# RWKV6 stage of a one-core hybrid layer: mixing on ACT and POOL, r times k on VectorE, other places for parts of PE's work and for the sends, the first fills from SBUF, weights from ACT's queue

## The chip, the core and the metric

The kernel runs on one core of a Trainium2 chip. Its engines are TensorE (PE, with its weight loads, PEld), VectorE (DVE), ScalarE (ACT), GpSimd (POOL) and SyncE (SP), which here only issues transfers. Each engine works through its own instructions in order; semaphores tie them together. The metric is the device time of one execution in microseconds, and lower is better.

## What is computed

The input x has 4 sequences of 1024 tokens with 256 channels, all in fp32. Four sublayers follow one another, each as `x = x + f(layernorm(x))`: a retention attention, a mixture of experts (MoE: 8 experts, the best two of a softmax router, SiLU-gated), an RWKV6 attention, and the same MoE with the same weights again. The change is in the RWKV6 sublayer and in its handover to the second MoE. Cut to what matters, RWKV6 is:

```
sx  = shift(x) - x                               # shift: the token before
m   = tanh((x + sx * maa_x) @ tm_w1)             # 5 parts of 32 columns
xf  = x + sx * (maa[f] + m[f] @ tm_w2[f])        # f = 0..4: w, k, v, r, g
r, k, v, g = x3 @ Wr, x1 @ Wk, x2 @ Wv, silu(x4 @ Wg)
w   = exp(-exp(decay + tanh(x0 @ td_w1) @ td_w2))
# for each of 16 heads (16 x 16 state), token by token:
y_t = r_t . (state + u * k_t v_t)
state = w_t * state + k_t v_t
out = (groupnorm(y) * ln_w + ln_b) * g @ Wo
```

The term `r . (u * k v)` does not need the state. The kernel computes it apart, as `bonus = v * sum(u * r * k)`.

## The kernel before

**Stages.** Retention comes first (0 to about 350 us of the profiled execution). The first MoE follows as two halves of 2048 tokens, 39 slots of 128 rows each. RWKV6's block 0 is prepared during the second half (`prepare`, lists `first`). RWKV6 then runs until about 1358 us. The second MoE ends the program.

**RWKV6.** The 4096 tokens are 8 blocks of 512 (`NBLK`, block j; two blocks make one sequence). In a block, 8 slots n = 0..7 of two runs h = 0, 1 cover the 256 x 16 state rows. This text counts slots over the whole stage too: slot 8j + n. For each run:

- `fill` (L926 to 937) brings the values of v, spread over partitions, from a DRAM copy (`v_all`, written by `store`, L915) into a tile `w_vb` (3 buffers), by SP's queue. It is issued two runs ahead.
- `run` (L951) is the core: on DVE a product k*v (L957, 128x1024) and two scans (L959, 128x512 each) that carry the state along 512 tokens; on POOL the product with r (L967). The tiles `w_s` have 6 buffers. Parts given as `between` go on DVE between the two scans.
- `sums` (L980) adds the state rows on PE into `w_yp`, one slot later.

`factors` (L908) makes the tile `w_wk` of one half g of the channels on ACT: `exp(-ew)` and a copy of k. Slots 0 to 3 use g = 0, slots 4 to 7 use g = 1 in the scans.

**The next block, in between.** While block j runs, block j+1 is prepared piece by piece: `normed`, `turn` (transposes; sx on POOL), `mix` (tanh), `both` (products `w_dp` on PE, L842, then `mixed`, L845 to 856, which makes each `w_xf`), `decay`, `decay2` and `projected` (L880). Block j-1 is finished at the same time: `centre`, `spread`, `root`, `spread_out`, `gated`, `out_part`, `added`. The lists `given`, `amid`, `late` and `uses` (L1074 to 1112) are written out by hand and say in which slot each part is emitted: `uses` between the scans of the slot's first run, `amid` after that run, `late` at the slot's end, and `given[n, h]` after the other run of slot n.

**The second MoE's router and rows.** For each finished block, `block` takes statistics, `logits` (L491) transposes the normed rows and multiplies with the router into `m_lp`, and `biased` (L504) adds the bias on DVE. `route` runs one of 8 pieces of small DVE operations that sort the rows to experts. `send` (L634) makes one tile of rows on ACT and scatters it to DRAM by two indirect DMAs of POOL. The main loop (L1367 to 1391) puts these into slots, and loads the expert weights `w1a` and `w2a` (4 and 2 MB, `load`, L1251) by SP's queue in the slots 58 to 63, after the pool `pi`, which held the tiles of RWKV6's preparation, has been released.

**Order.** PE and ACT, and in these stages DVE and POOL too, run in the order in which the program emits their instructions. Only SP's order, which holds nothing but transfers, is laid by a planner.

## Time and profile before

| | us |
|---|---|
| runs: median of 3 (lowest, highest) | 1650.17 (1642.9, 1650.6) |
| the profiled execution: its own time | 1690.56 |
| its span, from the first to the last instruction | 1688.7 |
| RWKV6: first to last running product and scan | 698.1 to 1358.1 |
| second MoE: first matmul on fetched rows | 1368.5 |

The profile shows one execution, and it took 2.4% longer than the median of the runs. Sums over its rows are therefore sums against 1690.56. A row of a group gives the line, the engine, the operation, the tiles, the shapes and the count, then the busy time and the mean of one in ns, then the idle time just before and what ended it. A row of the waits names who waited for whom, the total, the number of times and the longest. A row of the windows gives the busy time of each engine in a stretch of the span.

### The profile page before, as it was taken

The numbers are of one execution on the slowest core, as the hardware profiler recorded it, in microseconds if no ns is written. First come the engines' busy times: TensorE is split into PE (matmuls) and PEld (weight loads), VectorE is DVE, ScalarE is ACT, GpSimd is POOL, SyncE is SP. The second block draws the span as 40 slices with busy tenths as digits, with TensorE's granted clock in tenths as the row PEclk, the third lists the DMA queues.
The fourth block names the chain that finished last, engine by engine and source line by source line (L and its number), as shares of the span: only waits on it lengthen the run. The fifth ranks groups of instructions, "written<-read, shape, count | busy, mean of one in ns | idle before, by whom it ended". The sixth has DMA issues, their size and how long they took to land. (4 is left out here: it accounts for less than half of the span.)

```text
span 1688.7 us, 21332 instructions
## 1 busy us (share of the span) xinstructions
PE 1418.5 (84%) x6800; PEld 747.9 (44%) x6800; DVE 1002.8 (59%) x1874; ACT 608.8 (36%) x1451; POOL 925.2 (55%) x879
## 2 busy tenths in 40 slices
PE   6999998858989999888898889878876467989993
PEld 4666665635555555322333333323322134555662
DVE  6666556414323532597978897889976824423534
ACT  2343334323343333424343434432425133433331
POOL 4233323632455344698969696966797732464331
PEclk9999988879999999979878787877877758999997
DMA  8921111132333421666545343533445910333625
GB/s 305 334 67 51 55 47 54 62 113 74 98 118 124 145 65 56 152 161 152 148 112 137 98 128 98 137 88 93 119 119 144 270 58 32 101 123 123 207 92 174
DMA packets 111882, 204.11 MB, mean 121 GB/s; under 512 B 12224, under 2 KB 73632, under 8 KB 111776
## 3 DMA queue, kind: packets, MB, share of 16 engines
q1 hardware_dynamic: 93920, 161.07, 33.5%
q0 software_dynamic: 17856, 41.70, 7.9%
q8 instruction: 58, 0.95, 0.2%
q14 instruction: 48, 0.39, 0.1%
HBM read 142.27 MB, written 60.45 MB: 120 GB/s over the span
## 5 line engine op out<-in xcount | busy, mean ns | idle before, releaser
L967 POOL TENSOR_TENSOR w_s<-w_s,w_rT 128x1024 f32<-128x1024 f32 x128 | 304.2, 2394 | 92.3 <-DVE w_s L959 88.6
L708 POOL DMA_INDIRECT y_all<-m_y,m_to x156 | 151.0, 968 | 328.5 <-ACT m_xt L663 191.4
L668 PE MATMUL m_hp<-w1a,m_xt 128*128 x624 | 311.4, 623 | 11.7 <-ACT m_xt L663 10.3
L674 DVE TENSOR_TENSOR m_a<-m_hp,m_sg 128x256 f32<-128x256 f32 x156 | 66.2, 424 | 352.7 <-ACT m_sg L672 320.9
L702 PE MATMUL m_op<-w2a,m_aT 128*128 x624 | 165.2, 388 | 13.7 <-ACT m_y L707 11.2
L957 DVE TENSOR_TENSOR w_vb<-w_vb,w_wk 128x1024 f32<-128x1024 f32 x128 | 153.9, 1202 | 37.2 <-DMA w_vb<-v_all 20.9
L959 DVE TENSOR_TENSOR_SCAN w_s<-w_wk,w_carry,w_vb 128x512 f32<-128x512 f32 x128 | 160.2, 1275 | 7.8
L959 DVE TENSOR_TENSOR_SCAN w_s<-w_wk,w_vb 128x512 f32<-128x512 f32 x128 | 152.0, 1215 | 7.4
L668 PEld LDWEIGHTS m_hp<-w1a,m_xt 128*128 128x128 f32 x624 | 112.1, 200 | 94.6 <-issue 82.8
L640 POOL DMA_INDIRECT xg_all<-m_row,m_at x128 | 124.7, 974 | 51.9 <-issue 30.0
L672 ACT ACTIVATE m_sg<-m_hp 128x256 f32<-128x256 f32 x156 | 59.9, 384 | 174.2 <-PE m_hp L668 143.9
L707 ACT ACTIVATE m_y<-m_op,m_share 128x256 f32<-128x256 f32 x156 | 73.8, 473 | 133.4 <-PE m_op L702 85.4
L702 PEld LDWEIGHTS m_op<-w2a,m_aT 128*128 128x128 f32 x624 | 108.0, 193 | 28.7 <-ACT m_y L707 17.4
L297 POOL TENSOR_TENSOR a_t<-a_t,a_t 128x512 f32<-128x512 f32 x32 | 41.1, 1285 | 124.8 <-DVE a_t L296 114.7
L990 PE MATMUL w_yp<-w_s,core_c 128*32 128x512 f32 x512 | 91.0, 711 | 10.9 <-POOL w_s L967 10.7
L842 PE MATMUL w_dp<-w_m,tm_w2a 32*128 32x512 f32 x128 | 75.5, 837 | 17.3 <-DVE w_cen L1044 7.4
L856 POOL TENSOR_TENSOR w_xf<-w_xf,w_xT 128x512 f32<-128x512 f32 x80 | 86.1, 1091 | 4.2 <-DVE w_xf L852 0.4
L695 PEld LDWEIGHTS m_atp<-cst,m_a 128*128 128x128 f32 x312 | 44.1, 144 | 92.8 <-issue 74.0
L327 DVE TENSOR_TENSOR a_pt<-a_sp,ret_c 128x2048 f32<-128x2048 f32 x32 | 73.1, 2286 | 17.8 <-PE a_sp L324 17.7
L663 ACT COPY m_xt<-m_xtp 128x256 f32<-128x256 f32 x156 | 57.0, 366 | 48.5 <-PE m_xtp L659 45.9
L659 PE MATMUL m_xtp<-cst,m_xg 128*128 128x128 f32 x312 | 63.0, 286 | 13.5 <-DMA m_xg<-xg_all 13.0
L697 DVE COPY m_aT<-m_atp 128x256 f32<-128x256 f32 x156 | 64.9, 416 | 5.2 <-PE m_xtp L659 2.9
(226 smaller groups left out, 2480.1 us busy)
## 6 DMA issues: line engine op xcount, KB each, us to landing
w_vb<-v_all SPq DMA_DIRECT2D x128, 512.0 KB
m_xg<-xg_all SPq DMA_DIRECT2D x36, 520.0 KB
tab<-in_rope SPq DMA_DIRECT2D x32, 512.0 KB
m_back<-y_all SPq DMA_DIRECT2D x48, 256.0 KB
xg_all<-zero SPq DMA_DIRECT2D x18, 520.0 KB
w1a<-in_w SPq DMA_DIRECT2D x16, 512.0 KB
v_all<-w_vT SPq DMA_DIRECT2D x64, 128.0 KB
res<-in_x SPq DMA_DIRECT2D x8, 512.0 KB
```

What stands on the lines that cost most here:

```text
L327: nc.vector.tensor_mul(pts[i].rearrange("p j n t -> p (j n) t"), sp.rearrange("p j n t -> p (j n) t"), causal.unsqueeze(1).to_broadcast([P ...
L640: nc.gpsimd.indirect_dma_start(out=xg_views[self.half][2 * i + n][:, :], out_offset=bass.IndirectOffsetOnAxis(ap=self.at[n][:, i : i + 1], ...
L668: mm(hp, lhsT=self.xt[j][:, c, :], rhs=w1a[:, bass.ds(self.ev[j], 1), c, :].rearrange("p o n -> p (o n)"), start=(c == 0), stop=(c == KC - 1))
L702: mm(op, lhsT=self.aT[j][:, c, :], rhs=w2a[:, bass.ds(self.ev[j], 1), c, :].rearrange("p o n -> p (o n)"), start=(c == 0), stop=(c == KC - 1))
L707: nc.scalar.activation(y, op, AF.Copy, scale=self.share[g][:, i : i + 1])
L708: nc.gpsimd.indirect_dma_start(out=y_views[self.half][j][:, :], out_offset=bass.IndirectOffsetOnAxis(ap=self.to[g][:, i : i + 1], axis=0), ...
L842: mm(dp, lhsT=wt[rows, c * P : (c + 1) * P], rhs=m[rows, :], start=True, stop=True)
L856: nc.gpsimd.tensor_add(xf, xf, d["now"][:, c, :])
L957: nc.vector.tensor_mul(vb, vb, wk[:, 1:2, :].to_broadcast([P, 2, BLK]))
L959: nc.vector.tensor_tensor_scan(s[:, q, 1 : BLK + 1], wk[:, 0, :], vb[:, q, :], 0.0 if j % NB == 0 else st[j - 1]["carry"][:, n, 2 * h + q ...
L967: nc.gpsimd.tensor_mul(s[:, :, 0:BLK], s[:, :, 0:BLK], d["r"][:, g, :].unsqueeze(1).to_broadcast([P, 2, BLK]),)
L990: mm(d["yp", g][32 * q : 32 * q + 32, :], lhsT=w["sel"][:, i, :], rhs=d["s", n, q // 2][:, q % 2, 0:BLK], start=False, stop=(i == 3), skip ...
```

## The change

`mixed`: f = 0 and 2 no longer use one DVE instruction each (except for the last two blocks), but an activation on ACT and a product on POOL, as the other three do. `paired` is new: r times k is made on DVE, half by half, from the copy of k in `w_wk`, in place of one product on POOL at the end of `projected`. `logits` is split into `turned` (transposes) and `product` (router matmuls), the second placed three slots later, and `biased` one slot after that. Mixing of f = 4 moves from slot 6 to slot 7, `turn` from slot 6's end to slot 7's, `out_part 0` from slot 5's end to the middle of slot 6, and its `added` half a slot later. `begun` fills the first two `w_vb` of block 0 out of SBUF, ahead of the store. The constants of the end of a block (`tail_c`, `w_o`, `w_ln`) are loaded in the slots 1 to 4 of block 0 (`rwkv_last`); the emitted order is this, and SP's planner still puts ten of these small loads and `tail_c` ahead. The routing pieces stand four by four in the slots 44 and 45 (before: one in each of 42 to 49). The sends stand in the slots of `SENT` (before: one in each of 48 to 63). The expert weights are loaded by ACT's queue in the slots 58 to 61.

```diff
-        def logits(self, n):
-            tT = ph.tile([P, KC, BLK], F32, name="m_tT", tag="m_tT", bufs=1)
+        def turned(self, n):
+            tT = self.tT = ph.tile([P, KC, BLK], F32, name="m_tT", tag="m_tT", bufs=1)
             xn = [ph.tile([P, C], F32, name="m_xn", tag="m_xn", bufs=4) for i in range(NT)]
...
                 across(lambda i: xn[i], m, tT[:, :, 2 * m * P : (2 * m + 2) * P], "m_")
+        def logits(self, n):
+            self.turned(n)
+            self.product()
+        def product(self):
+            tT = self.tT
             lp = self.lp = psum([P, NT, E], "m_lp")
...
                     maa, sx = vec[:, c, V_MAA + f : V_MAA + f + 1], d["sx"][:, c, :]
-                    if f in (0, 2):
+                    if f in (0, 2) and j >= NBLK - 2:
                         nc.vector.scalar_tensor_tensor(xf, dp, maa, sx, ALU.add, ALU.mult)
...
                     nc.scalar.copy(o[:, m, :], pp)
-            if n == "r":
-                d["rk"] = full(pcs, "w_rk", 1)
-                nc.gpsimd.tensor_mul(d["rk"], d["k"], o)
+        def paired(j, g):
+            d = st[j]
+            d["rk", g] = half(pcs, "w_rk")
+            nc.vector.tensor_mul(d["rk", g], d["wk", g][:, 1, :], d["r"][:, g, :])
         def own(j, g):
...
             cp = d["cp"] = psum([P, BLK], "w_cp")
-            mm(cp, lhsT=w["sum"][:, g, :], rhs=d["rk"][:, g, :], start=True, stop=True)
+            mm(cp, lhsT=w["sum"][:, g, :], rhs=d["rk", g], start=True, stop=True)
...
             vb = d["vb", n, h] = pcs.tile([P, 2, BLK], F32, name="w_vb", tag="w_vb", bufs=3)
+            if j == 0 and m < 2:
+                for q in range(2):
+                    row = 32 * (2 * h + q) + GH * i
+                    nc.sync.dma_start(
+                        out=vb[:, q, :],
+                        in_=d["v"][row : row + GH, g, :].unsqueeze(1).to_broadcast([GH, D, BLK]),
+                    )
+                return
             row = 64 * h + 2 * GH * i
...
+        def begun(j):
+            for m in range(2):
+                fill(j, m)
+            store(j)
         def ready(j, n, h):
...
             [],
-            [(0, decay2), (0, projected, "v", 2), (0, store), (0, projected, "k", 1),
+            [(0, projected, "v", 2), (0, begun), (0, decay2), (0, projected, "k", 1),
              (0, both, [(4, 0), (4, 1)])],
...
             (4, 0): [(3, 1), (2, 1)],
-            (6, 1): [(4, 0), (4, 1)],
+            (7, 0): [(4, 0), (4, 1)],
         }
...
             5: [(1, projected, "k", 1), (2, normed)],
-            6: [(1, projected, "v", 2)],
+            6: [(-1, out_part, 0), (1, projected, "v", 2)],
             7: [(1, projected, "r", 3), (1, factors, 0)],
...
             4: [(-1, spread_out, 1)],
-            5: [(-1, out_part, 0)],
-            6: [(1, store), (-1, out_part, 2), (0, centre, 0), (2, turn)],
-            7: [],
+            5: [],
+            6: [(1, store), (-1, out_part, 2), (0, centre, 0)],
+            7: [(2, turn)],
         }
         uses = {
-            0: [],
-            1: [(0, bonus, 0)],
-            2: [(0, bonus, 1)],
-            3: [(-1, root)],
-            4: [(-1, gated, 0)],
-            5: [(-1, gated, 1)],
-            6: [(-1, added, 0)],
-            7: [(-1, added, 2)],
+            (0, 0): [(0, paired, 0)],
+            (1, 0): [(0, bonus, 0)],
+            (1, 1): [(0, paired, 1)],
+            (2, 0): [(0, bonus, 1)],
+            (3, 0): [(-1, root)],
+            (4, 0): [(-1, gated, 0)],
+            (5, 0): [(-1, gated, 1)],
+            (6, 1): [(-1, added, 0)],
+            (7, 0): [(-1, added, 2)],
         }
...
                 factors(0, 0)
-                for m in range(2):
-                    filled(m)
             for h in range(2):
                 filled(2 * n + h + 2)
-                run(j, n, h, at(uses[n], j) + middle if h == 0 else ())
+                run(j, n, h, at(uses.get((n, h), ()), j) + (middle if h == 0 else []))
                 mixing(1 - h)
...
             else:
-                do([p for p in uses[n] + late[n] if p[0] == -1], NBLK)
+                if n == 6:
+                    out_part(NBLK - 1, 0)
+                    added(NBLK - 1, 0)
+                parts = uses.get((n, 0), []) + late[n]
+                do([p for p in parts if p[0] == -1], NBLK)
...
         after = pct.tile([P, N_TAIL], F32, name="tail_c")
-        nc.sync.dma_start(out=after, in_=consts[:, A_TAIL:N_CONST])
+        w["after"] = after
...
         w["o"] = pct.tile([P, KC, C], F32, name="w_o")
-        ln = pct.tile([P, KC, N_VEC], F32, name="w_ln")
-        for q in range(4):
-            for i in range(4):
-                rows = slice(32 * q + GH * i, 32 * q + GH * (i + 1))
-                nc.sync.dma_start(
-                    out=w["o"][rows, :, :],
-                    in_=w_o.rearrange("(g h n) c -> n h g c", g=KC, n=D)[4 * i + q],
-                )
-                nc.sync.dma_start(
-                    out=ln[rows, :, :],
-                    in_=vecs.rearrange("(h n) (k m) -> n h k m", n=D, k=KC)[4 * i + q],
-                )
+        w["ln"] = ln = pct.tile([P, KC, N_VEC], F32, name="w_ln")
         w["lnw"], w["lnb"] = ln[:, :, V_LNW : V_LNW + 1], ln[:, :, V_LNB : V_LNB + 1]
...
+    def rwkv_last(w, q):
+        if q == 0:
+            nc.sync.dma_start(out=w["after"], in_=consts[:, A_TAIL:N_CONST])
+        for i in range(4):
+            rows = slice(32 * q + GH * i, 32 * q + GH * (i + 1))
+            nc.sync.dma_start(
+                out=w["o"][rows, :, :],
+                in_=w_o.rearrange("(g h n) c -> n h g c", g=KC, n=D)[4 * i + q],
+            )
+            nc.sync.dma_start(
+                out=w["ln"][rows, :, :],
+                in_=vecs.rearrange("(h n) (k m) -> n h k m", n=D, k=KC)[4 * i + q],
+            )
...
-    def load(t, src, experts=range(E)):
+    def load(t, src, experts=range(E), eng=nc.sync):
         for e in experts:
-            nc.sync.dma_start(out=t[:, e, :, :], in_=src[e].rearrange("(k p) n -> p k n", p=P))
+            eng.dma_start(out=t[:, e, :, :], in_=src[e].rearrange("(k p) n -> p k n", p=P))
...
     rwkv_rest(w)
-    for n in range(8, 10):
-        prepare(n)
+    prepare(8)
+    prepare(9)
     back, next_a, next_b = moes[0][1], moes[1][0], moes[1][1]
...
     extra, mids = {}, {}
+    SENT = (46, 48, 50, 52, 54, 55, 56, 57, 57, 58, 58, 59, 59, 60, 60, 61)
     for i in range(2 * HB):
...
     for i in range(HT):
-        add(48 + i, next_a.send, i)
+        add(SENT[i], next_a.send, i)
     for n in range(2 * HB - 1):
...
         add(8 * n + 15, m.block, n % HB)
-        add(8 * n + 16, m.logits, n % HB)
-        mids[8 * n + 17] = [(m.biased, n % HB)]
+        add(8 * n + 16, m.turned, n % HB)
+        add(8 * n + 19, m.product)
+        mids[8 * n + 20] = [(m.biased, n % HB)]
     for n in range(PIECES):
-        add(42 + n, next_a.route)
+        add(44 + n // 4, next_a.route)
     for j in range(NBLK):
...
             wstep(j, n, mids.get(8 * j + n, []))
+            if j == 0 and 1 <= n <= 4:
+                rwkv_last(w, n - 1)
             for f, *a in extra.get(8 * j + n, ()):
...
                 w1a, w2a = room(pw2)
-            if j == NBLK - 1 and n > 1:
-                some = range((n - 2) * E // 6, (n - 1) * E // 6)
-                load(w1a, w1, some)
-                load(w2a, w2, some)
+            if j == NBLK - 1 and 2 <= n < 6:
+                for t, src in ((w1a, w1), (w2a, w2)):
+                    load(t, src, range(2 * (n - 2), 2 * (n - 1)), nc.scalar)
     finish(0)
```

## The prediction

> **What bounds the kernel now.** I read the page's busy shares first. No engine is full over the whole span, so the stages have to be read apart.
>
> ```profile
> PE 1418.5 (84%) x6800; PEld 747.9 (44%) x6800; DVE 1002.8 (59%) x1874; ACT 608.8 (36%) x1451; POOL 925.2 (55%) x879
> ```
>
> Nearly all edits lie in the RWKV6 stage. I cut the span at the first running product (L957) of each of its eight blocks and asked for the busy time of each stretch. Columns: stretch, length, busy time of PE, PE's weight loads, DVE, ACT, POOL, TensorE clock, DMA share, GB/s.
>
> ```profile
> 698.10:764.50 66.40, 55.24 (x161) 16.73 (x160) 61.26 (x63) 22.48 (x48) 62.36 (x59) 0.82 0.71 170
> 764.50:843.70 79.20, 63.79 (x209) 21.43 (x208) 69.71 (x81) 29.10 (x63) 71.00 (x47) 0.89 0.61 145
> 926.00:1007.80 81.80, 71.56 (x233) 27.21 (x232) 70.00 (x82) 32.27 (x69) 65.38 (x46) 0.83 0.42 115
> 1089.40:1193.30 103.90, 80.52 (x253) 29.57 (x251) 95.02 (x123) 33.49 (x72) 70.59 (x51) 0.80 0.33 92
> 1193.30:1274.70 81.40, 62.46 (x206) 23.66 (x206) 68.38 (x77) 32.48 (x73) 69.95 (x64) 0.81 0.47 127
> 1274.70:1358.10 83.40, 43.21 (x158) 16.10 (x160) 63.23 (x62) 22.77 (x58) 60.45 (x40) 0.69 0.74 195
> ```
>
> Blocks 0, 1, 3, 5, 6, 7 are shown; 2 and 4 look like 3. DVE is the fullest or nearly so in blocks 0 to 5. What it does in the rest is in the table of its waits (us in total, times, longest):
>
> ```profile
> DVE w_xf L852 <- PE w_dp L842: 22.3, 10, 3.6
> DVE w_vb L957 <- DMA w_vb<-v_all: 20.9, 7, 15.4
> DVE res L224 <- PE w_op L219: 13.7, 6, 6.8
> DVE m_logit L505 <- PE m_lp L501: 10.8, 5, 5.4
> DVE w_vb L957 <- issue: 9.4, 1, 9.4
> DVE w_vb L957 <- ACT w_wk L913: 6.9, 4, 2.7
> ```
>
> With two smaller rows (4.7, 4.1) they sum to 92.8, and 563.5 busy with 92.8 waiting make the 660 us from 698.1 to 1358.1. So **DVE's in-order stream sets the stage**. It never waits on POOL, whose largest wait is on DVE (w_s L967, 88.6). Half of DVE's waits are on PE. The timelines of PE and DVE at the start of block 3, and then of ACT, show how:
>
> ```profile
> 934.12 3.46 PE L501 MATMUL m_lp<-wr,m_tT 128*128 128x8 f32 x16
> 937.52 2.07 PE L842 MATMUL w_dp<-w_m,tm_w2a 32*128 32x512 f32 x2
> 942.54 0.75 DVE L852 SCALAR_TENSOR_TENSOR w_xf<-w_dp,vec,w_sx 128x512 f32<-128x512 f32 x1 [3.54 <-PE w_dp L842]
> 951.40 0.59 ACT L913 COPY w_wk<-w_kT 128x512 f32<-128x512 f32 x1
> ```
>
> The router's 3.46 us on PE stand ahead of the product that DVE waits for. The last row is the second w_wk, ready 26.0 into the block; today slot 4 is the first to read it. In block 7, SP's waits:
>
> ```profile
> SPq L1253 <- PE w_pp L886: 19.8, 1, 19.8
> ```
>
> and two 5 us windows after it, columns as above:
>
> ```profile
> 1300.00:1305.00 5.00, 4.71 (x44) 1.58 (x42) 0.00 (x0) 4.94 (x12) 1.01 (x1) 1.00 1.01 277
> 1345.00:1350.00 5.00, 1.45 (x12) 0.22 (x12) 4.90 (x5) 2.23 (x6) 4.16 (x3) 1.00 1.04 270
> ```
>
> SP stood 19.8 us at the first weight load, until PE had left the room it goes to; fills of w_vb stood behind it, and DVE had 9.4 us of nothing. Then DMA is full until 1350 at some 268 GB/s. The next MoE starts at 1368.5, when its first rows (fetch at 1364.8, behind POOL's last sends of 1360.8 and 1362.1) have landed.
>
> **What the Trainium skill says.** "DMA: Bandwidth & Descriptors", Issuing engines are not separate DMA queues: loads issued by ACT and SP use the same 16 engines. The full DMA from 1300 to 1350 fits. Same page, Queues, rings and completion order: an engine goes round robin between queues with work, so a fill need not stand behind all weights issued earlier; no row here shows it, as all came from SP. "SBUF — State Buffer", Who interferes with whom: a DVE instruction with two SBUF inputs and a POOL one that reads SBUF exclude each other. L957 is such a one and stays within 1186 to 1223 ns, so the product moved to DVE is charged nothing for it; the other end is a POOL product (2.39) for each of 16, 38 us.
>
> **The change, part by part.** S is a block's start.
>
> *Mixing of f=0 and 2.* In blocks 0 to 4 DVE loses 20 x 0.736 = 14.7 us. ACT gets 20 x 0.68 = 13.6, hidden (under 40% busy). POOL gets 20 x 1.295 (L855) = 25.9. Block 0's own four run ahead of 698.
>
> *r times k.* POOL loses 7 x 2.48 (L894) = 17.3 in the stage; DVE gets 16 halves. Half of L957 is 0.60, L1044 takes 0.66: 0.62 each, 9.9. So DVE goes from 563.5 to 558.7, POOL from 532.4 to 541.0.
>
> *The new wait.* paired reads w_wk: the second one is now wanted in slot 1. DVE's own stream gets there at S + 14.9 (three runs of 3.7, two of 0.65, then 1.3 + 1.2). When is it ready? Mixing of g, moved to slot 7, and sx behind it put 4.7 + 1.9 on POOL ahead of the router's statistics (1.7): out at about S + 9.5, today S + 5.5. m_xn and transposes: S + 12. No router follows, so w_dp starts there (today S + 11.5). From w_dp to the second w_wk block 1, which has no router, took 772.2 to 781.9 = 9.7; block 3 took 14.5. So S + 21.7, 4.3 earlier than today, but DVE waits 6.8 (0 to 11). Behind it, DVE's second scan; PE's own and sums stand too.
>
> *Blocks 2 to 4.* After 21.7: product 0.6, scan 1.2, run 2.5, bonus 0.6, scan 1.2 put the second run of slot 2 at S + 27.8; today it is S + 28.2 (954.2). So the w_xf and m_logit waits (5.6 in block 3) are mostly turned into the new one. Later in the block: two L852 1.5, res 0.9 (out_part 0 half a slot later, behind z), root 0.6, w_wk 0.5 (w_r comes ahead of g's mixing). -4 each: **-12**. POOL would have 68 of 78 us.
>
> *Blocks 0 and 1.* The second w_wk is in time in block 0 (S + 13); POOL's 133.4 + 10.4 - 5.0 = 138.8 of 145.6 leaves little: **-2.5**.
>
> *Routing in slots 44 and 45.* L631 and L632, 2.5 us, go from block 6 to 5, and a piece follows at once on PE's ranking that it needs: 0 to 6, I take 3. Block 5 keeps its L852: slot 2 at S + 29.3 against 26.5. 2.8 + 2.5 + 3 - 0.3: **+8**. Block 6: slot 2 at 29.3 against 24.2, +5.1; res loses 8 of 8.8, others 1: **-4**. POOL loses three sends there (six of 0.99) and rk.
>
> *Sends.* Ten lie in slots 56 to 61: POOL has 2 x 2 + 4.7 in slots of 8, lags some 5 us and recovers in the last two. The fetch no longer waits for them.
>
> *Weights by ACT.* 16 issues of 0.55 (SP's: 0.40 to 1.07) = 9 us, hidden in an ACT 27% busy; behind them stand rows to send and carries. SP's 19.8, DVE's 9.4 and its 5.4 for m_logit go. Fills share engines with weights and sends: 5 us of waits left (0 to 20). Block 7: slot 2 half done at 27.8, eleven runs 40.7, root, gated, added 4.5, fills 5 = 78, PE's sums 4.6: MoE at S + 82.6. The bytes bind as well: from S + 31.5, 6.3 MB weights + 5.5 fills + 1.9 sends at 268 GB/s take 51: S + 82.5. Against 93.8: **-11.2**.
>
> *First fills from SBUF, constants later.* The first run waited for its fill until 698.1, but w_wk ended at 697.6: **-0.4**. 22 small loads now stand between SP's later fills at 0.3 each, covered by three fill buffers. *finish*: out_part 0 and added stand together in one MoE tile: **+1.5**.
>
> Sum: -12 - 2.5 + 8 - 4 - 11.2 - 0.4 + 1.5 = -20.6. The profiled execution took 1690.6 (span 1688.7), the median of the runs is 1650.17, 2.4% less. 1690.6 - 20.6 = 1670.0, times 0.976: **1630**.
>
> **Rivals.** *The new wait stays small* (more gain): if POOL has the statistics out as early as today, w_wk comes 4 us earlier in blocks 2 to 7, 24 in all: -45, 1606.[...] Against: POOL's order.
> *POOL's lag reaches DVE* (slower): in slots 3 to 5 of block 3 POOL idles 2 us in 25, and two added products come there. A lag L at the block's end delays statistics, m_xn, w_dp, w_wk and so DVE, in blocks 1 to 7: 7 L. From L = 3 the gain is gone; at 6 it is -20.6 + 42 = +21, 1671. Against: 541 us of work in 635, and slots 0 and 1 let POOL recover.
> *Fills late in block 7*: weights in four slots instead of six, fills wait 20 instead of 5: -6, 1644.
> *It does not do what it says*: the first fills, at 0.4, are that.
>
> **How the numbers follow.** Forecast 0.52 (its own range 1618 to 1642), small wait 0.20, POOL's lag 0.14, late fills 0.14. A measurement tells about 0.5% (8 us) from none. Faster 0.52 + 0.19 + 0.03 = 0.74; same 0.01 + 0.02 + 0.10 = 0.13; slower 0.13. Range 1603 to 1656, leaving out most of POOL's case and the end of the small wait.
>
> **What would show it.** Right: DVE waits on ACT's w_wk by 5 to 9 us in each of blocks 2 to 6, m_logit and the 9.4 gone, blocks 2 to 4 at 76 to 80, MoE 80 to 85 after block 7's start. Wrong: no such wait, blocks at 74; or blocks of 84, the statistics on POOL later than S + 13; or w_vb late by over 10 us in block 7.

## The result, and the profile after

The changed kernel takes 1644.44 us (median of 20 runs, 1638.3 to 1657.6), the kernel before 1656.16 (20 runs beside them). The ratio is 0.9942, 95% interval 0.9919 to 0.9964: faster by 0.4 to 0.8%, where 1.2% was forecast. The sign was right and the size a little under half.

Beside the experiments below, run on other chips, the kernel before takes 1686 to 1688. So kernels are compared by their ratio, and by one stretch of the profile that hardly moves between executions: from the first running product of RWKV6 to the first rows of the second MoE. It took 670.4 and 670.3 in two profiles of the kernel before, 659.0 and 659.8 in two of the kernel after: 11.0 us less, close to what the ratio says (0.58% of 1656 is 9.6). The time of the first product itself followed the execution, not the kernel (679 and 703 in two profiles of the same changed kernel). What the stretch leaves out at its start is small: from the first MoE's last product to the first running product it is 17.9 and 18.9 us before, 17.4 in both profiles after.

The busy shares of the page:

```profile
PE 1393.2 (85%) x6800; PEld 735.2 (45%) x6800; DVE 985.0 (60%) x1866; ACT 624.5 (38%) x1475; POOL 936.4 (57%) x895
```

They say little. The span cut at the first product of each block (now L979) says where the time went. Columns: stretch, length, busy time of PE, PE's weight loads, DVE, ACT, POOL, TensorE clock, DMA share, GB/s. The rows are blocks 0, 1, 3, 5, 6 and 7:

```profile
679.23:760.54 81.31, 60.13 (x168) 18.08 (x167) 60.02 (x61) 24.91 (x54) 67.31 (x61) 0.79 0.72 161
760.54:842.00 81.46, 67.64 (x211) 22.41 (x209) 68.16 (x78) 31.48 (x64) 72.26 (x50) 0.85 0.64 147
...
921.28:1000.89 79.61, 65.40 (x236) 24.67 (x232) 68.07 (x81) 34.46 (x72) 68.11 (x49) 0.87 0.44 118
...
1081.21:1179.98 98.77, 75.87 (x252) 27.30 (x244) 87.52 (x129) 34.53 (x73) 65.42 (x47) 0.83 0.38 101
1179.98:1257.36 77.38, 66.44 (x216) 24.53 (x216) 66.81 (x76) 30.97 (x67) 69.24 (x64) 0.78 0.50 131
1257.36:1334.01 76.65, 45.03 (x158) 17.60 (x160) 64.62 (x65) 24.31 (x62) 66.39 (x49) 0.71 0.75 220
```

The next table has the mean of two profiles each (before and after), with the prediction's terms beside them. A single block repeats less well than the whole stretch: in the two profiles before, block 1 takes 79.2 and 81.8, block 7 with the handover 93.8 and 91.3.

| us | before | after | change | forecast |
|---|---|---|---|---|
| blocks 0 and 1 | 66.0 + 80.5 | 81.2 + 81.5 | +16.2 | -2.9 |
| blocks 2 to 4 | 82.5, 81.8, 81.6 | 79.5, 79.9, 80.3 | -6.3 | -12 |
| block 5 | 103.9 | 98.7 | -5.2 | +8 |
| block 6 | 81.4 | 77.4 | -4.1 | -4 |
| block 7 and handover | 92.6 | 80.9 | -11.6 | -11.2 |

The waits of DVE over the stage (us in total, times, longest):

```profile
DVE w_rk L904 <- ACT w_wk L922: 44.5, 7, 8.1
DVE w_vb L979 <- DMA w_vb<-v_all: 24.8, 12, 5.7
...
DVE w_xf L859 <- PE w_dp L849: 3.9, 3, 2.0
DVE w_s L981 <- ACT w_carry L999: 3.9, 1, 3.9
DVE w_vb L979 <- DMA w_vb<-w_vT: 3.2, 1, 3.2
```

The first row is the new wait that was forecast, one in each of blocks 1 to 7. The m_logit row of the blocks and the 9.4 us in block 7 are gone, and w_xf fell from 22.3 to 3.9. The timeline of block 3 shows how it comes about:

```profile
928.76 1.04 POOL L193 TENSOR_TENSOR m_rstd<-m_ve,mhalf 128x4 f32<-128x4 f32 x1
930.32 2.08 ACT L486 ACTIVATE m_xn<-res,m_shift,m_rstd 128x256 f32<-128x256 f32 x4 [2.10 <-POOL m_shift L204]
933.08 2.08 PE L849 MATMUL w_dp<-w_m,tm_w2a 32*128 32x512 f32 x4
943.69 0.59 ACT L922 COPY w_wk<-w_kT 128x512 f32<-128x512 f32 x1
944.31 0.69 DVE L904 TENSOR_TENSOR w_rk<-w_wk,w_rT 128x512 f32<-128x512 f32 x1 [8.10 <-ACT w_wk L922]
```

POOL has the statistics out 9.0 us into the block (921.28 to 930.29), w_dp starts at 11.8, the second w_wk is ready at 23.0, and DVE has stood 8.1 us for it. The forecast had 9.5, 12, 21.7 and 6.8 for these four.

What was not forecast is in block 0. The first row is from the kernel before, the others from the changed one:

```profile
687.68 5.57 SPq L920 DMA_DIRECT2D v_all<-w_vT  x8
...
674.57 14.49 SPq L929 DMA_DIRECT2D v_all<-w_vT  x8
686.61 1.22 DVE L979 TENSOR_TENSOR w_vb<-w_vb,w_wk 128x1024 f32<-128x1024 f32 x1 [3.19 <-DMA w_vb<-w_vT]
694.02 1.22 DVE L979 TENSOR_TENSOR w_vb<-w_vb,w_wk 128x1024 f32<-128x1024 f32 x1 [3.81 <-DMA w_vb<-v_all]
743.41 2.07 ACT L804 ACTIVATE w_xn<-res,w_shift,w_rstd 128x256 f32<-128x256 f32 x4 [9.08 <-POOL w_xT L808]
745.66 2.34 DVE L981 TENSOR_TENSOR_SCAN w_s<-w_wk,w_vb 128x512 f32<-128x512 f32 x2 [3.90 <-ACT w_carry L999]
751.17 1.22 DVE L979 TENSOR_TENSOR w_vb<-w_vb,w_wk 128x1024 f32<-128x1024 f32 x1 [3.17 <-DMA w_vb<-v_all]
760.54 1.22 DVE L979 TENSOR_TENSOR w_vb<-w_vb,w_wk 128x1024 f32<-128x1024 f32 x1 [5.68 <-DMA w_vb<-v_all]
```

These are two groups of waits. At the start, the store of v (8 issues) takes SP 14.5 us behind the fills out of SBUF, where it took 5.6 before (first row); the second run waits for its SBUF fill, the third for the first fill behind the store. At the end, ACT stands 9.1 us for POOL's statistics of block 2; behind it in ACT's order are a carry and the copy of v that block 1's store and fills need.

Block 5 is the other surprise: DVE is busy 87.5 us in it instead of 95.0, with six instructions more. The timeline of POOL and then of DVE in slot 44:

```profile
1131.21 4.66 POOL L989 TENSOR_TENSOR w_s<-w_s,w_rT 128x1024 f32<-128x1024 f32 x2
1135.82 1.32 POOL L862 TENSOR_TENSOR w_xf<-w_xf,w_sx 128x512 f32<-128x512 f32 x1
1133.64 2.37 DVE L537 TENSOR_TENSOR m_eq<-m_logit,m_top 128x128 f32<-128x128 f32 x1
1136.05 1.24 DVE L538 TENSOR_TENSOR m_eq<-m_eq,cst 128x128 f32<-128x128 f32 x1
1139.91 0.29 DVE L537 TENSOR_TENSOR m_eq<-m_rest,m_top 128x128 f32<-128x128 f32 x1
1140.23 0.29 DVE L538 TENSOR_TENSOR m_eq<-m_eq,cst 128x128 f32<-128x128 f32 x1
```

The same two operations take 2.37 and 1.24 us beside POOL and 0.29 each once POOL has nothing left. The first ends at 1136.01, where POOL's second product ends (1135.87); the other at 1137.29, where POOL's next operation ends (1137.14).

### The profile page after: what moved, and what is told of

Read it like the earlier page. It is cut to its first block, busy times and chain, and to the rows that moved or that the text cites. A ratio compares the mean times of both kernels' runs of the same rounds, so it can differ in the third digit from the quotient of the medians.

```text
span 1646.6 us, 21369 instructions
## 1 busy us (share of the span) xinstructions
PE 1393.2 (85%) x6800; PEld 735.2 (45%) x6800; DVE 985.0 (60%) x1866; ACT 624.5 (38%) x1475; POOL 936.4 (57%) x895
## 4 chain that ended last, share of the span: by engine, by line
PE 53%; DVE 16%; POOL 14%; ACT 7%; DMA 4%; issue 4%; SPq 2%; DVEq 0%; POOLq 0%; ACTq 0%
PE m_hp L675 16%; PE m_op L709 8%; DVE w_s L981 6%; POOL w_s L989 5%; PE w_pp L893 3%; PE a_qkp L285 3%; DMA w_vb<-v_all 3%; DVE w_vb L979 3%; POOL w_xf L862 2%; PE m_xtp L666 2%; PE a_yp L344 2%; PE m_lp L508 2%; POOL w_xf L863 2%; PE m_atp L702 2%; PE a_gp L267 2%
## 5 line engine op out<-in xcount | busy, mean ns | idle before, releaser
L979 DVE TENSOR_TENSOR w_vb<-w_vb,w_wk 128x1024 f32<-128x1024 f32 x128 | 153.6, 1200 | 42.9 <-DMA w_vb<-v_all 24.8
L981 DVE TENSOR_TENSOR_SCAN w_s<-w_wk,w_vb 128x512 f32<-128x512 f32 x128 | 152.8, 1216 | 11.2 <-ACT w_carry L999 3.9
L675 PEld LDWEIGHTS m_hp<-w1a,m_xt 128*128 128x128 f32 x624 | 111.5, 199 | 93.3 <-issue 79.5
L862 POOL TENSOR_TENSOR w_xf<-w_xf,w_sx 128x512 f32<-128x512 f32 x72 | 91.9, 1276 | 9.0 <-ACT w_xf L861 8.6
L327 DVE TENSOR_TENSOR a_pt<-a_sp,ret_c 128x2048 f32<-128x2048 f32 x32 | 73.2, 2286 | 16.3 <-PE a_sp L324 16.2
L861 ACT ACTIVATE w_xf<-w_dp,vec 128x512 f32<-128x512 f32 x72 | 47.0, 684 | 70.7 <-PE w_dp L849 70.6
L666 PE MATMUL m_xtp<-cst,m_xg 128*128 128x128 f32 x312 | 62.5, 284 | 10.4 <-DMA m_xg<-xg_all 9.9
```

The costliest lines, as they stand in the source:

```text
L666: nc.tensor.transpose(tp[:, c, :], self.xg[j // GRP][:, j % GRP, c * P : (c + 1) * P], ident)
L675: mm(hp, lhsT=self.xt[j][:, c, :], rhs=w1a[:, bass.ds(self.ev[j], 1), c, :].rearrange("p o n -> p (o n)"), start=(c == 0), stop=(c == KC - 1))
L862: nc.gpsimd.tensor_mul(xf, xf, sx)
L979: nc.vector.tensor_mul(vb, vb, wk[:, 1:2, :].to_broadcast([P, 2, BLK]))
L981: nc.vector.tensor_tensor_scan(s[:, q, 1 : BLK + 1], wk[:, 0, :], vb[:, q, :], 0.0 if j % NB == 0 else st[j - 1]["carry"][:, n, 2 * h + q ...
```

## The experiments

"Stretch" is that from the first product to the second MoE. Unless said otherwise the kernel altered is the changed one, and each edit undoes one thing or moves one.

| run | stretch, us | ratio to the kernel before | 95% interval |
|---|---|---|---|
| kernel before (two profiles) | 670.4, 670.3 | 1 | |
| changed kernel; again (after_2) | 659.0; 659.8 | 0.9942; 0.9953 | 0.9919-0.9964; 0.9934-0.9973 |
| a_fills | 653.2 | 0.9906 | 0.9869-0.9943 |
| b_mix1 | 659.1 | 0.9909 | 0.9873-0.9945 |
| d_pair2 | 633.4 | 0.9781 | 0.9740-0.9822 |
| f_three | 616.8 | 0.9708 | 0.9672-0.9745 |
| g_sp | 659.5 | 0.9951 | 0.9934-0.9968 |
| h_route | 666.8 | 0.9980 | 0.9955-1.0005 |
| i_router | 680.0 | 1.0077 | 1.0052-1.0102 |
| j_mix | 651.6 | 0.9886 | 0.9861-0.9911 |
| k_rk | 654.9 | 0.9892 | 0.9832-0.9952 |
| l_sends | 669.9 | 1.0024 | 1.0004-1.0043 |
| m_four | 612.6 | 0.9643 | 0.9595-0.9691 |
| n_sp_router | 680.3 | 1.0064 | 1.0047-1.0080 |
| o_before_router | 646.1 | 0.9911 | 0.9880-0.9943 |

**The references**, both kernels again.

> The kernel before, unchanged, for a second profile. In the two profiles the stretch before the first running product is 18.9 us shorter after the change and the second MoE 11.8 us shorter, though neither holds any changed work but block 0's preparation. If that is one execution's chance, this profile has the first product near 680 us, 308 to 312 us from the first rows of the second MoE to the end, and 665 to 672 us between (670.4 in the first profile). If the change shortens those stretches, they stay near 698 and 320.

The first product is at 698.8, the stretch takes 670.3, and 320.9 us follow from the second MoE's first rows to the end. Taken alone that reads as if the change shortened what lies outside the stretch. But the changed kernel, run again on such a chip (1687 us for the kernel before), has its first product at 702.7. The second MoE takes 315.4 there, and from 316 to 323 in the kernels altered below: that is too wide to say whether the change does anything to it.

> The changed kernel again, as the reference for the kernels beside it. If the gain is made in RWKV6 and its handover alone, the profile has 659 us from the first running product to the first rows of the second MoE, as in its first profile (659.0), against 670.4 and 670.3 in two profiles of the kernel before, and the ratio is 0.993 to 0.995. If the chance of one execution made it, the stretch differs by several us.

The stretch is 659.8 us and the ratio 0.9953, as expected. The stretch repeats to within 1 us.

**a_fills: the first fills.**

```diff
         def begun(j):
+            store(j)
             for m in range(2):
                 fill(j, m)
-            store(j)
# fill: no branch for j == 0 and m < 2
```

> The changed kernel with block 0's first two fills again out of the DRAM copy, behind the store, which stays behind the projection of v (now the first part of the last preparation). Theory: the fills out of SBUF hold SP's queue and with it the store (8 issues over 14.5 us instead of 5.6), so the second and third run wait 3.2 and 3.8 us; without them the first run is no later, the two waits go and block 0 takes some 74 us instead of 81.3: 7 us less, near 1637. Rival: VectorE and POOL have other work that ends block 0 anyway (POOL is 96% busy in it from 711 us on), and the gain is under 2 us.

Block 0 took 74.3 us (81.2 in the changed kernel), the stretch 653.2: 6.2 less, close to the theory's 7. The first run still waits for w_wk (14.9 us), not for its fill: with v's projection ahead of decay2, the store and a fill behind it come in time without the way through SBUF. The waits at the block's end stay (4.0, 3.0, 6.0).

**b_mix1: mixing of blocks 0 and 1 on DVE.**

```diff
-                    if f in (0, 2) and j >= NBLK - 2:
+                    if f in (0, 2) and (j <= 1 or j >= NBLK - 2):
```

> The changed kernel with the mixing of f = 0 and 2 of blocks 0 and 1 on VectorE as before; blocks 2 to 5 stay on ACT and POOL. Theory: POOL's lag ends block 0 (ScalarE waits 9.1 us for it with block 2's normed rows, and behind them stand the copy of v for block 1's store and a carry); POOL gets back 4 x 1.295 = 5.2 us, VectorE takes 4 x 0.74 = 2.9, block 0 becomes 3 to 6 us shorter and the time about 4 us less. Rival: only the late first fills make block 0 long; then VectorE's 2.9 us show and the time rises by 0 to 3.

The stretch stays at 659.1 us. Block 0 takes 79.5, which is 1.7 shorter and less than the theory's 3; the carry's wait is gone, but w_rk and w_xf now wait 2.8 and 1.9 there. Neither the ratio nor the block's length tells the two theories apart. POOL's statistics of block 2 are out 64.0 us into block 0, and 64.2 in the changed kernel: POOL is done with them 5.6 us after DVE's part instead of 13.5, but DVE's part comes 7.6 us later. So ACT stands for them no shorter (11.0 us, 9.1 in the changed kernel), and whether POOL's lag ends the block is not tested here.

**d_pair2: r times k one slot later.**

```diff
-            (1, 1): [(0, paired, 1)],
-            (2, 0): [(0, bonus, 1)],
+            (2, 1): [(0, paired, 1)],
             (3, 0): [(-1, root)],
+            (3, 1): [(0, bonus, 1)],
# late: own(0, 1) from slot 1 to slot 2
```

> The changed kernel with the second half of r times k one slot later (between the scans of slot 2's second run), its product on TensorE at the end of slot 2, its bonus in slot 3's second run. Nothing is added or taken away. Theory: VectorE's wait for the second w_wk (44.5 us, 7 times) is the main bound of blocks 1 to 7; it goes, and 15 to 35 of it are gained, the rest turning into waits for w_xf, w_op or a fill: 1610 to 1630. Rival: POOL, with some 70 us of work in blocks of 79, is the bound behind it; then under 8 us are gained and VectorE waits elsewhere by the same amount.

The stretch takes 633.4 us, 26 less, in the middle of the theory's range; blocks 2 to 4 take 74.6 to 76.1. Its waits of DVE:

```profile
DVE w_varp L1048 <- ACT q_y L1040: 15.1, 7, 4.3
...
DVE w_xf L859 <- PE w_dp L849: 7.5, 5, 2.1
...
DVE w_rk L904 <- ACT w_wk L922: 1.7, 1, 1.7
```

The 44.5 us are down to 1.7; some 20 came back as other waits (w_varp 15.1 instead of 6.0, w_xf 7.5 instead of 3.9, res and m_logit). POOL, with as much work as before, was not the bound.

**g_sp and n_sp_router: the weights' queue.**

```diff
-                    load(t, src, range(2 * (n - 2), 2 * (n - 1)), nc.scalar)
+                    load(t, src, range(2 * (n - 2), 2 * (n - 1)))
```

> The changed kernel with the 16 weight loads of the last block on SP's queue again, in the same four slots. Theory: they stand in SP's order until TensorE has left the room that they go to, fills of w_vb stand behind them, and VectorE waits 8 to 12 us in block 7 as it did before: 89 to 92 us from block 7's start to the first rows of the second MoE instead of 80.8, the time up by 8 to 11. Rival: the bytes bind (weights, fills and sends share the DMA engines), or the gain of block 7 came from the earlier sends and the router's place; then it stays within 80 to 83.

The stretch takes 659.5 us, and 80.9 pass from block 7's start to the second MoE. My theory fell. SP's own wait for the room in block 7 of g_sp:

```profile
SPq L1282 <- PE w_pp L893: 5.7, 1, 5.7
```

SP stands 5.7 us instead of 19.8: the first load is issued 18.7 us into the block instead of 24.1 (22.6 in n_sp_router, where the router stands on PE ahead of w_pp again), and six of the block's fills have been laid ahead of it instead of four. DVE waits for no fill at all.

> The changed kernel with two things as before: the weight loads on SP's queue (alone no change: 659.5) and the router's matmuls straight behind the transposes (alone 680.0). Theory: SP's stand in the kernel before needed both a room that comes free late and few fills laid ahead; with the router back the room is free near 22 us into block 7, six fills stand ahead and cover it for some 19 us, so VectorE waits at most 3 us for fills in block 7 and the stretch is 680 to 683. Rival: the queue matters as soon as the room is late; VectorE waits 6 to 11 us in block 7 and the stretch is 686 to 692.

The stretch takes 680.3 us with the router back as well, no different from i_router (680.0): SP stands 3.7 us, six fills are laid ahead again, and DVE waits for none in block 7. The queue that issues the loads brought nothing in either setting. That agrees with the Trainium skill, "DMA: Bandwidth & Descriptors", Issuing engines are not separate DMA queues: another issuer saves issue time, not bandwidth.

**i_router: the router's product straight behind its transposes.**

```diff
-        add(8 * n + 16, m.turned, n % HB)
-        add(8 * n + 19, m.product)
-        mids[8 * n + 20] = [(m.biased, n % HB)]
+        add(8 * n + 16, m.logits, n % HB)
+        mids[8 * n + 17] = [(m.biased, n % HB)]
```

> The changed kernel with the router's matmuls again straight behind their transposes (and the bias in the slot after), as before. Theory: TensorE's order sets when the second w_wk comes: 3.5 us of router stand ahead of the product w_dp in blocks 2 to 7, the wait of VectorE grows by about that in each, and the room for the weights comes free 3 to 5 us later in block 7. The stretch from the first product to the second MoE goes from 659.4 (mean of two profiles) to 674 to 684. Rival: POOL's late statistics and ScalarE's chain set w_wk and TensorE has room; then it stays within 659 to 664.

The stretch takes 680.0 us, 20.6 more, as the theory had it, but through other rows:

```profile
DVE w_rk L904 <- ACT w_wk L922: 40.6, 7, 7.3
DVE m_logit L512 <- PE m_lp L508: 26.2, 6, 5.7
```

The wait for w_wk does not grow. m_logit stands between the scans of slot 1's first run, ahead of it in DVE's order, so DVE waits there first for the same late PE, 4.4 us in each of six blocks, and then again as long as before.

**o_before_router: that place alone, in the kernel before** (the edit above the other way round; routing pieces in slots 44 to 51).

> The kernel before with only the router's matmuls moved three slots later (the bias four; the routing pieces one in each of the slots 44 to 51, as they need the last bias). Theory: this place is what carries the change. In blocks 2 to 7 the 3.5 us of router no longer stand ahead of w_dp, VectorE's waits for w_xf and m_logit (5 to 8 us a block) go, and in block 7 the room for the weights is free some 4 us earlier: 12 to 25 us less, 645 to 658 from the first product to the second MoE instead of 670.3, and the ratio 0.985 to 0.993. Rival: without r times k on VectorE nothing of that order waits for w_wk, other waits take the place of these, and under 5 us are gained (666 to 671).

The stretch takes 646.1 us, 24 less than the kernel before and 13 less than the whole change. The ratio (0.991) says 10 to 20 us and puts it less far ahead of the whole change (0.9942, 0.9953); the profiled execution is the fastest of this kernel's five, so 24 is an upper end. Blocks 2 to 4 take 74.6 to 76.4 instead of 81.6 to 82.5. So the router's place carries the change, and what stands beside it takes away more than it adds. What it does not mend is the waiting for fills in block 7:

```profile
DVE w_vb L964 <- DMA w_vb<-v_all: 12.4, 4, 11.6
...
SPq L1260 <- PE w_pp L893: 19.0, 1, 19.0
```

The loads stand here in six slots, as before, and only three of block 7's fills are laid ahead of the first one.

**j_mix: mixing of f = 0 and 2 on DVE in all blocks.**

```diff
-                    if f in (0, 2) and j >= NBLK - 2:
+                    if f in (0, 2):
```

> The changed kernel with the mixing of f = 0 and 2 on VectorE in all blocks, as before. Theory: VectorE's stream sets the stage, but the first of its four operations in a block stands ahead of the wait for w_wk and is hidden in it: 3 x 0.74 = 2.2 us more in each of blocks 2 to 5, nothing over blocks 0 and 1 together (as in the kernel that did this for them alone), so 666 to 670 us from the first product to the second MoE (659.4). Rival: the 5.2 us that POOL gets back in each block let its statistics and products come earlier and pay for it; then 655 to 661.

The stretch takes 651.6 us, 7.8 less than the changed kernel: the rival's side, and beyond its range. Block 1:

```profile
779.47:854.91 75.44, 61.90 (x206) 20.10 (x205) 70.68 (x82) 28.69 (x59) 65.82 (x45) 0.89 0.67 154
```

Six of the 8 us are here: POOL has 65.8 us of work instead of 72.3 and the block takes 75.4 instead of 81.5, although DVE has 2.5 us more. Blocks 3 and 4 stay at 80.3 and 80.0 with 2.7 us more on DVE, and its waits are shorter by as much. Block 4 shows it, first in the changed kernel and then in j_mix:

```profile
1023.41 0.69 DVE L904 TENSOR_TENSOR w_rk<-w_wk,w_rT 128x512 f32<-128x512 f32 x1 [8.03 <-ACT w_wk L922]
...
1036.76 0.69 DVE L904 TENSOR_TENSOR w_rk<-w_wk,w_rT 128x512 f32<-128x512 f32 x1 [5.47 <-ACT w_wk L922]
```

DVE comes to this wait 14.5 us into the block and then 17.2, and goes on at 22.5 and 22.7. POOL's statistics are out at 9.1 in both, so it is not an earlier POOL that pays here. The wait for w_wk is 34.2 us over the stage instead of 44.5. That b_mix1 did not gain has the same reason: it gave POOL nothing back in block 1, which mixes block 2.

**k_rk: r times k on POOL again.**

```diff
                     nc.scalar.copy(o[:, m, :], pp)
+            if n == "r":
+                d["rk"] = full(pcs, "w_rk", 1)
+                nc.gpsimd.tensor_mul(d["rk"], d["k"], o)
# uses: both paired entries taken out
```

> The changed kernel with r times k as one product on POOL at the end of the projection of r, as before; VectorE's two halves are gone, and with them its wait for the second w_wk. Theory: the wait was the cost of this edit, and VectorE also loses 1.36 us a block: 624 to 636 us from the first product to the second MoE, at least as good as placing the halves a slot later (633.4). Rival: POOL's 2.4 us at the block's end stand ahead of the statistics and the sums, and VectorE waits for w_dp or a fill instead: 640 to 652.

The stretch takes 654.9 us, 4.5 less; both ranges missed. DVE's waits:

```profile
DVE w_bonus L917 <- PE w_cp L912: 24.2, 6, 7.5
...
DVE w_xf L859 <- PE w_dp L849: 14.7, 4, 5.9
DVE w_varp L1050 <- ACT q_y L1042: 11.6, 5, 3.4
```

w_wk is waited for no more, but the second bonus, one slot on, now waits for PE, whose product w_cp stands behind the projection of g. So the wait is not the price of w_wk alone: what feeds the second half of the bonus comes some 20 us into a block on PE and ACT, and whoever asks in slot 1 or 2 pays. d_pair2 moved the whole chain (product, w_cp, bonus) and gained over five times as much. Block 1 is as short here (76.1) as in j_mix, with POOL busy 73.5 us in it: POOL's load alone does not set that block.

**l_sends: one send in each of the slots 48 to 63.**

```diff
-    SENT = (46, 48, 50, 52, 54, 55, 56, 57, 57, 58, 58, 59, 59, 60, 60, 61)
+    SENT = tuple(range(48, 64))
```

> The changed kernel with one send in each of the slots 48 to 63, as before. Theory: the second MoE's first rows wait for POOL's last sends: from the last scan to them some 10 us as before (10.1 to 10.4) instead of 4.4, while blocks 6 and 7 gain up to 3 from a lighter POOL: the stretch to the second MoE 662 to 666 instead of 659.4. Rival: the weights and fills set the first rows; then no change (658 to 661).

The stretch takes 669.9 us, 10.5 more. From the last scan to the second MoE it is 10.4 us instead of 4.4, as expected; and block 6 takes 82.5 instead of 77.4, which was not expected (res waits 4.5 us for w_op there). POOL and SP at the end of l_sends:

```profile
1365.39 1.01 POOL L647 DMA_INDIRECT xg_all<-m_row,m_at  x1 [0.16 <-issue]
1366.70 0.96 POOL L647 DMA_INDIRECT xg_all<-m_row,m_at  x1 [0.30 <-issue]
1369.43 0.95 SPq L658 DMA_DIRECT2D m_xg<-xg_all  x2
```

The fetch follows 1.8 us after the last send. In after_2 the last send ends at 1350.99 and the fetch starts at 1356.95; SP's last wait there is for PE's sums.

**h_route: the routing pieces apart.**

```diff
-        add(44 + n // 4, next_a.route)
+        add(44 + n, next_a.route)
# the first two sends in slots 48 and 49
```

> The changed kernel with the eight routing pieces one in each of the slots 44 to 51 instead of four and four in 44 and 45 (the first two sends go to slots 48 and 49, since they need the fourth piece). Theory: a VectorE operation with two operands in SBUF stands still while POOL works through a product; a separate piece starts beside one and pays for it (operations of 0.17 to 0.4 us took 1.0 to 2.4 in the kernel before), a bunch pays once and then runs beside an idle POOL. Then blocks 5 and 6 together need 5 to 10 us more VectorE time and get that much longer (176.2 now). Rival, the prediction's: the pieces cost the same wherever they stand, and bunched ones wait for TensorE's ranking besides; then blocks 5 and 6 together get 0 to 5 us shorter.

Blocks 5 and 6:

```profile
1099.97:1200.69 100.72, 72.66 (x245) 27.15 (x237) 89.97 (x117) 33.41 (x70) 68.46 (x50) 0.80 0.38 100
1200.69:1282.50 81.81, 68.70 (x226) 23.39 (x224) 74.87 (x87) 31.77 (x69) 66.35 (x62) 0.83 0.46 122
```

DVE is busy 164.8 us over the two (154.3 in the changed kernel) with as many routing operations, and they take 182.5 instead of 176.1. The theory was right: the pieces apart cost DVE 10.5 us more, of which 6.4 show in the length of these two blocks.

**f_three and m_four: placed again.** f_three joins the edits of a_fills and d_pair2 and one more:

```diff
-            5: [(1, projected, "k", 1), (2, normed)],
-            6: [(-1, out_part, 0), (1, projected, "v", 2)],
+            5: [(1, projected, "k", 1)],
+            6: [(-1, out_part, 0), (1, projected, "v", 2), (2, normed)],
```

> The changed kernel with three places altered: first fills behind the store, the second half of r times k a slot later, and the layernorm of the block after next behind the projection of v (slot 6) instead of ahead of it (slot 5). Theory: the first two bring 5.8 and 25.6 us as they did alone; with the third ScalarE no longer stands before POOL's statistics with v's copy behind it, block 1's store and fills come in time, and the waits at block 0's end (4.0, 3.0 and 6.0 us in the kernel with the first alone) mostly go: 6 to 11 more. The stretch from the first product to the second MoE is 616 to 623 us instead of 659. Rival: the layernorm is then late for the transposes at slot 7's end and for the mixing of the next block; the third place brings nothing or costs up to 8 (628 to 636).

The stretch takes 616.8 us, within the theory's range. Block 0 takes 67.1 (74.3 in a_fills): ACT now copies v before it stands for POOL. The 7.2 us are a difference of two kernels; the third place was not run alone.

> The kernel with three places altered (first fills, second half of r times k, layernorm), and in addition the mixing of f = 0 and 2 on VectorE in all blocks. In the changed kernel that alone brought 8.2 us, since VectorE's time was hidden in its wait and POOL was full in block 1. Theory: with the wait gone VectorE's stream binds again, and 4 x 0.74 = 2.9 us come back in each of blocks 0 to 4: 625 to 631 us from the first product to the second MoE, against 616.8. Rival: POOL's stream still ends the blocks; then 5.2 us less of it in each bring 3 to 8 in all: 609 to 614.

The stretch takes 612.6 us, in the rival's range. Both theories hold in part: blocks 0 and 1 gain 3.2 and 5.8, and blocks 2 to 4 lose 3.5, 1.8 and 1.0, since without the wait part of DVE's 2.9 us does show there.

```profile
DVE w_xf L859 <- PE w_dp L849: 19.4, 12, 2.3
...
DVE w_vb L971 <- DMA w_vb<-v_all: 1.5, 2, 0.8
```

The fills hardly wait any more. At 0.9643 (0.9595 to 0.9691) m_four is the fastest of all kernels here, 3.6% ahead of the kernel before.

## Why the prediction was half right

Two terms of the sum failed, in opposite directions. Blocks 0 and 1 with the first fills were put at -2.9 and came at +16.2: the prediction followed a transfer to its first user only, and charged nothing for POOL's load there. Block 5 was put at +8 and came at -5.2: the routing operations were priced at what they took before. The errors of +19 and -13 cancel in part, so it is also luck that the sum kept its sign: without the second error the stretch would have gained nothing. That 1644 is also the number of the rival of late fills is chance: DVE waits 3.1 us for fills in block 7, not 20.

**The new wait: right** in place, chain and size: 6.8 forecast, 6.4 measured on the average of seven. What the forecast took for granted is that the kernel had to have it: d_pair2 asks one slot later and is 26 us shorter.

**Blocks 2 to 4, -4 each: -2.1 each.** The step that credited DVE with the work taken off it was wrong in kind. Work of DVE ahead of its wait only shortens that wait, and work behind it was taken up by later waits: j_mix puts the mixing back and blocks 3 and 4 stay where they are. What these blocks gained is the router's place (i_router: 3 to 4 us a block), less the new wait. One sum under it was off as well: 563.5 busy and 92.8 waiting are 656, not 660, and the 15.4 us of the first fill lie ahead of the stage. Some 19 us of the stage are in no row of its waits. That DVE's stream sets the stage still holds.

**Blocks 0 and 1, -2.9: +16.2. The worst term.** The first fills were put at -0.4, since only the first run was looked at; SP's order behind them was not followed. They cost 6.2 (a_fills). That POOL "leaves little" was seen and then priced at nothing: the mixing done in block 1 costs 6 (j_mix, and 5.8 between f_three and m_four). The end of block 0, where ACT stands for POOL with v's copy behind it, was not looked at; between a_fills and f_three it gets 7 us shorter. The rival of POOL's lag saw a real thing. From DVE's part of the statistics of the block after next to the end of POOL's it was 5.0 to 6.3 us in blocks 0 to 4 before; it is 13.5 in block 0, 10.3 in block 1 and some 9 in blocks 2 to 4. But the router's statistics came at 9.0 in block 3, not after 13 as that rival had it, and blocks 2 to 4 did not become longer.

**Block 5, +8: -5.2.** The operations that moved were priced at what they took before. The prediction cited the Trainium skill, "SBUF — State Buffer", Who interferes with whom, and then charged nothing, because L957 runs undisturbed beside POOL. That was a wrong witness: its operand w_wk comes from a pool of PSUM banks, so it has one input in SBUF. Some of the routing operations have two, and they pay up to 2.4 us for 0.29. Bunched, they pay mostly at the bunch's start: 6.4 us over blocks 5 and 6 (h_route). The 3 us charged for PE's ranking did not come either (m_cnt waits 0.2). The rest of the 13 is not told apart. The price could be read before: most of the 2.5 us that were carried into block 5 is one operation, here in the kernel before and then in the changed one.

```profile
1200.75 2.35 DVE L632 TENSOR_TENSOR m_else<-cst,m_else 128x39 f32<-128x39 f32 x1
...
1161.83 0.20 DVE L639 TENSOR_TENSOR m_else<-cst,m_else 128x39 f32<-128x39 f32 x1
```

The first stood beside a product of POOL's that ended with it (1203.04 and 1203.09); the same line took 0.20 in the first MoE.

**Block 6, -4: -4.1**, in sum right; its parts were not told apart.

**Block 7 and handover, -11.2: -11.6, with a wrong cause inside.** SP's stand and DVE's 9.4 and 5.4 went as forecast, but not through ACT's queue (g_sp: nothing). The 9.4 went with more fills laid ahead of the loads: n_sp_router has the late room and SP's queue, and no waits for fills; o_before_router has the early room, the loads in their old slots, and 12.4 us of them. Which edit makes the planner lay six ahead was not tested; the loads' four slots are the nearest. The 5.4 for m_logit is the router's place (i_router: 5.7 back, block 7 and handover 84.8). The sends gave the handover's 6 (l_sends).

**finish, +1.5**: not told apart; it lies in the second MoE, whose length differs by more from chip to chip.

The sum: -22.1 for the stretch was forecast, -11.0 came. The errors are +19 (blocks 0 and 1), +6 (2 to 4), -13 (block 5) and -0.4 (block 7). Undone one at a time the edits are worth -21 (router), -10 (sends), -7 (routing), 0 (queue), +6 (first fills), +8 (mixing), +5 (r times k). These do not add up to -11; that several of them pay into or hide in the same wait is the likely reason, not one that was shown. The new places of g's mixing, of the transposes, of out_part 0 and of the late constants were not undone alone.

## What to carry to other kernels

When an edit adds a wait to an in-order stream, what the edit saves on that stream ahead of it turns into more waiting, as long as what is waited for does not come sooner; price the wait first, and move its whole chain (here product, matmul and bonus) to where its input is ready. For each transfer put ahead of others in a queue, follow the queue to the next user, not only to the first. Work moved to an engine that has room on average (POOL, 57% busy over the span) can still delay what others wait for: look in each block at how late that engine comes to such work, not at its mean.

## What the hardware showed

- A DVE operation with two inputs in SBUF stood until POOL's operation was through: m_eq on 128x128 took 2.37 us beside a product of 2.3 and 0.29 without, and ended with it. A reduction (m_top, 0.27 beside such a product, 0.29 without) and a copy out of PSUM (m_cnt, 0.28 beside one in the kernel before, 0.29 without in the changed one) did not stand. Nor did a product with one input in PSUM: 19 of the 128 of L979 lie wholly beside a product of POOL's and take 1.19 to 1.22 us, like the rest. That is the rule of the page cited above (the Trainium skill, "SBUF — State Buffer", Who interferes with whom), with its price in this kernel.
- A cast of 128x39 from fp32 to int32 in SBUF stood as well, with one input: 1.73 us beside POOL's product and 0.48 in the kernel before, each time ending as POOL's operation ended (1159.83 and 1159.79, 1178.50 and 1178.46). Whoever looks at two-input operations alone would miss it.
